# A third recursion level for two more products in one pair of round P2, and three pairs of stores moved between DMA queues

## The chip, the cores and the metric

The kernel runs on one core of a Trainium2 chip. The time is device microseconds of one execution, and the median of several executions is what counts. The engines are named as in the profile: PE is the matrix engine (PEld its weight loads), DVE the vector engine, ACT the scalar engine, POOL the GpSimd engine, and SP the engine that only issues DMA transfers and waits. SP and ACT issue DMAs into queues of their own. An engine works through its instructions in program order, so an instruction that waits holds everything behind it on that engine.

## The reference

All arithmetic is float32, for 32 samples `x[b]` of 128 channels by 2048 positions:

```python
att   = softmax(mlp(cond_128))                          # (32, 8)
x0    = einsum('boi,bih->boh', att @ weight, x) + bias   # a mixed 128x128 kernel per sample
x     = x + x0 @ W.T + bias + sum_e w_e (x0 @ A_e.T) @ B_e.T   # 2048 x 2048, low-rank update
x2    = grouped_conv1d(x, 9 taps) + ctx
x     = x + unperm(down(gelu(up(perm(x2)))))             # 16 heads, 128 -> 512 -> 128
```

The low-rank update is folded into the weights, so that the largest product is 4096 rows (samples times channels) by a 2048 x 2048 weight. The change is within this product.

## The kernel before

**The big product** is done with the Winograd form of Strassen's algorithm, which needs seven products of half-size blocks instead of eight. There are two levels everywhere and a third level in places.

- The outer level is the order of work: seven **rounds** `ROUNDS = ("P1", "P2", "P6", "P7", "P5", "P3", "P4")`. A round runs over eight groups of samples, `g = 0..7`; one round and one group is a **step** (`i` counts steps). Steps 2p and 2p+1 are **pair** p. In a step the left operand is a block of `x` (or a sum of blocks, made on POOL by `x_combine`, tiles `xt` and `s_P`), and the right operand is a block of the weights (`w` or `wo_P`, and sums `P_t` of it, made by `inner_weights`).
- The second level is within a step: again seven products P1 to P7, each of four matmuls with a 128 x 128 stationary block and 512 moving columns. Each float32 matmul is two passes of PE, and the profile counts passes.
- The third level takes the inner products of the two steps of a pair together, as seven **quarter** products, each of four matmuls of 256 columns. `multiply_third` does this for the inner products P2 and P4 (one family of quarters): each step has five full products (P1, P5, P6, P3, P7), and the seven quarters stand in the odd step. `multiply_more` does it for P3 and P7 as well (a second family): each step has three full products (P1, P5, P6), four quarters stand in the even step and ten in the odd one.

`PAIRS` says which pairs of a round use the third level at all, and `MORE` which of them use it for the second family also. Per pair, the matmuls are thus:

| | full matmuls (512 columns) | quarter matmuls (256 columns) |
|---|---|---|
| `multiply_third` | 2 x 5 x 4 = 40 | 7 x 4 = 28 |
| `multiply_more` | 2 x 3 x 4 = 24 | 14 x 4 = 56 |

**What a second family costs on other engines.** `more_weights` makes two tiles `P_v` of weight sums, eight operations on POOL at the step ahead of the pair (L471), and eight on DVE (L1321), of which one is taken at each of the first four calls of `between` in two steps. `more_inputs` makes a tile `sv` of sums of `s_P` tiles, four operations on POOL (L481 to L484). Each quarter of the second family is added to the results by two DVE instructions instead of one:

```python
part = acc[:, :, n, cols]
nc.vector.tensor_tensor(part, ps.rearrange("p (s n) -> p s n", s=2), part, ALU.add)   # L538
if n:                                   # second family
    part = acc[:, 1, 0, cols]
    nc.vector.tensor_tensor(part, ps[:, NQ : 2 * NQ], part, ALU.add)                  # L543
```

**Between the products** of a step the function `between(j)` is called for j = 0 to 5. It places other DVE work there, above all the **mixes**: the 256 operations (32 samples by 8 experts) that make the mixed kernels `ags` (L725, L727). `MIXES[r][g]` is how many are placed at each of j = 0 to 3, so a 2 means eight in the step. They must add up to 64. Small work of the conditioning network (`small`, L1049 to L1176) is spread over the steps by `next(chain)`; its softmax is L1074 to L1083, with an Exp on ACT (L1078) in the middle of a DVE sequence, and it is placed at the end of step 3 of round P1.

**Round P1** has no earlier sums to add to: ACT copies the first results from PSUM (L602), DVE adds the others, and at the end of a pair the two result tiles `m_P` (1 MB each) are stored to `p_d`. The same round finishes the weights (`w_make_two`, L232 to L235): before each of its first six steps' products there are PE products with DVE sums on top, stored by ACT (L177).

**The order on the DMA queues** is the program's order. The queue of SP holds all loads of `x` (L277), of partial sums (`part_load`, L282) and of weights (L173, L688), and the stores of partial sums (`part_store`, L286) of every round but the first. Loads of `x` stand one step ahead in the first round and two steps ahead later. All large tiles share 26 slots of 8 KB per partition (pool `big`); a load waits until the slot that it gets has been let go.

Of the kernel before, what the change touches and what calls it, by code (L numbers as in the profile page):

```python
# [51 lines left out]
    "P1": (0, 1, 2, 3), "P2": (0, 1, 2, 3), "P6": (0, 1, 2, 3), "P7": (0, 1, 2, 3),  # L52
    "P5": (0, 1, 2, 3), "P3": (0, 1, 2, 3), "P4": (0,),
}
MORE = {"P6": (1,), "P7": (1, 2, 3), "P3": (1, 2, 3)}
MIXES = {
    "P1": (0, 0, 0, 0, 0, 0, 2, 5),
    "P2": (0, 2, 2, 2, 2, 2, 2, 2),
    "P6": (0, 2, 1, 2, 2, 2, 2, 2),
    "P7": (0, 2, 1, 2, 1, 2, 2, 1),  # L60
    "P5": (0, 0, 0, 1, 1, 2, 2, 2),
    "P3": (0, 2, 1, 2, 1, 2, 2, 1),
    "P4": (0,) * 8,
}
# [5 lines left out]
def adaln_ffn_kernel(  # L70
# [16 lines left out]
    nc = tc.nc  # L87
# [8 lines left out]
    def slot(name, shape=(P, L)):  # L96
        return big.tile(list(shape), FP, name=name, tag="s")


    def bank():  # L100
        return banks.pop(0)

    def done(*ps):
        banks.extend(ps)

    def halves(t):
        return [t[:, r * NQ : (r + 1) * NQ] for r in range(2)]
# [177 lines left out]
    def part_store(n, g, t, eng=nc.gpsimd):  # L285
        eng.dma_start(part_d[n, g], t.rearrange("p k s c -> p (k s c)"))  # L286
# [164 lines left out]
    def sums_rest(eng, n=4):  # L451
        for _ in range(min(n, len(rest))):
            eng.tensor_tensor(*rest.pop(0))

    def more_weights(name, rhs):

        quarters, ops = [], []
        for i, k in enumerate(("P3", "P7")):
            t = slot(f"{name}_v{i}", (P, 4, 2, NQ))
            q = {"P1": [], "P2": [], "P3": [], "P4": [], "P5": [], "P6": [], "P7": []}  # L460
            for kc in range(2):
                (r11, r12), (r21, r22) = (halves(rhs[k][2 * h + kc]) for h in range(2))
                for n, r in zip(q, (r11, r21, r22, t[:, 3, kc], t[:, 0, kc], t[:, 1, kc], t[:, 2, kc])):
                    q[n].append(r)
                ops += [
                    (t[:, 0, kc], r12, r11), (t[:, 1, kc], r22, t[:, 0, kc]),
                    (t[:, 2, kc], r22, r12), (t[:, 3, kc], r21, t[:, 1, kc]),
                ]
            quarters.append(q)
        for op in ops[:8]:  # L470
            nc.gpsimd.tensor_tensor(*op, ALU.subtract)  # L471
        return quarters, ops[8:]

    def more_inputs(i):

        (x11, x12), (x21, x22) = (
            [ss[n][:, 2:4, h * NQ : (h + 1) * NQ] for h in range(2)] for n in (i, i + 1)
        )
        tt = nc.gpsimd.tensor_tensor
        t = slot(f"sv_{i}", (P, 4, 2, NQ))  # L480
        tt(t[:, 0], x21, x22, ALU.add)  # L481
        tt(t[:, 1], t[:, 0], x11, ALU.subtract)
        tt(t[:, 2], x11, x21, ALU.subtract)
        tt(t[:, 3], x12, t[:, 1], ALU.subtract)  # L484
        return {
            "P1": x11, "P2": x12, "P3": t[:, 3], "P4": x22,
            "P5": t[:, 0], "P6": t[:, 1], "P7": t[:, 2],
        }

    def in_more(r, g):  # L490
        return g // 2 in MORE.get(r, ())

# [95 lines left out]
    def multiply_third(r, g, lhs, rhs, olds, between, quarters, sq):  # L588

        px, py = bank(), bank()  # L590
        accs = olds if olds[0] is not None else [slot(f"m_{r}{g}", (P, 2, 2, QW))]
        fresh = set()
        if sq:
            both = [held.pop(), accs]

        def add(si, oi, ps):
            for acc in accs:
                to = acc[:, si, oi]
                if olds[0] is not None or (si, oi) in fresh:
                    nc.vector.tensor_tensor(to, ps, to, ALU.add)  # L600
                else:
                    nc.scalar.copy(to, ps)  # L602
            fresh.add((si, oi))

        def product(k, ps, first, last):
            for kc in range(4):
                nc.tensor.matmul(  # L607
                    ps, lhsT=lhs[k][:, bass.ts(kc, P)], rhs=rhs[k][kc],
                    start=first and kc == 0, stop=last and kc == 3, skip_group_check=True,
                )  # L610

        def quarter(k, to):

            if k in ("P1", "P5", "P2"):
                qs[k] = bank()
            ps = qs[{"P6": "P1", "P7": "P1", "P4": "P1", "P3": "P5"}.get(k, k)]
            first, last = k in ("P1", "P2", "P5"), k in ("P2", "P3", "P4")
            for i, out in enumerate(halves(ps)):
                for kc in range(2):
                    nc.tensor.matmul(  # L620
                        out, lhsT=sq[k][:, i, bass.ts(kc, P)], rhs=quarters[i][k][kc],
                        start=first and i == 0 and kc == 0, stop=last and i == 1 and kc == 1,
                        skip_group_check=True,
                    )
            b, h = to
            for acc in both[b]:
                part = acc[:, :, 0, h * NQ : (h + 1) * NQ]
                nc.vector.tensor_tensor(
                    part, ps.rearrange("p (s n) -> p s n", s=2), part, ALU.add
                )  # L630
            if last:
                done(ps)

        qs = {}
        turns = [
            (("P1", (0, 0)), ("P2", (0, 0))), (("P6", (0, 1)), ("P5", (1, 1))),
            (("P7", (1, 1)), ("P3", (0, 1))), (("P4", (1, 0)),),
        ]

        def turn(n, now):  # L640
            if sq and now:
                for k, to in turns[n]:
                    quarter(k, to)

        early = r not in ENDS
        product("P1", px, True, False)
        add(0, 0, px)
        between(0)
        turn(0, early)
        if sq:  # L650
            sums_rest(nc.vector)
        product("P5", py, True, False)
        add(1, 1, py)
        between(1)
        turn(1, early)
        product("P6", px, False, False)
        add(0, 1, px)
        between(2)
        turn(2, early)
        product("P3", py, False, True)  # L660
        add(0, 1, py)
        done(py)
        between(3)
        turn(3, early)
        product("P7", px, False, True)
        add(1, 1, px)
        add(1, 0, px)
        done(px)
        turn(0, not early)
        between(4)  # L670
        turn(1, not early)
        turn(2, not early)
        between(5)
        turn(3, not early)
        if not sq:
            held.append(accs)
            return
        for b, accs in enumerate(both):
            for (_, new), acc in zip(ADDED[r], accs):
                part_store(new, g - 1 + b, acc, nc.scalar if r == "P1" else nc.sync)  # L680

    held = []

# [552 lines left out]
    for i, (r, g) in enumerate(steps):  # L1236
        ri = i // NG
        last_round = ri + 1 == len(ROUNDS)
        if i + 1 < len(steps):
            if i + 1 not in xs:  # L1240
                xs[i + 1] = x_loads(*steps[i + 1])
            if not last_round:
# [8 lines left out]
                if in_more(r, g) and g % 2 == 0:  # L1251
                    sv = more_inputs(i)
                if r in MORE and g == 2 * MORE[r][0] - 1:
                    more, more_ops = more_weights(r, rhs)
# [91 lines left out]
        if in_more(r, g):  # L1346
            multiply_more(
                r, g, lhs.pop(i), rhs, olds.pop(i), between, ((quarters, sq), (more, sv))
            )
        elif in_pair(r, g):  # L1350
            multiply_third(
                r, g, lhs.pop(i), rhs, olds.pop(i), between, quarters, sq if g % 2 else None
            )
        else:
            multiply(r, g, lhs.pop(i), rhs, olds.pop(i), between)
# [105 lines left out]
```

## Time and profile before

| | us |
|---|---|
| median of three executions | 2571.3 (2570.91 to 2572.54) |
| profiled execution | 2569.07 |
| its span, first to last instruction | 2567.3 |
| PE busy in the span | 2556.8, in 7238 passes |
| DVE busy | 1616.1 |
| POOL busy | 1411.2 |
| ACT busy | 532.2 |
| HBM traffic over the span | 224 GB/s |

The page gives the busy time of each engine, the share of it in 40 slices, the DMA queues and the costliest groups of instructions. The busy time of PE includes the overlap of pipelined passes, so that the pace of PE is better read from the starts of instructions in the timeline: the start of one row to the start of the next. Times in the text are microseconds from the start of the span. Round P1 ends at about 295, round P2 covers 295 to 481, and its pair 2 (steps 4 and 5) 388 to 435.

### The profile page before, as it was taken

Reading aid. Unit: us, or ns where it says so; the run is one execution under the profiler, and the core shown is the slowest. Engines: PE = TensorE matmul, PEld = TensorE weight load, DVE = VectorE, ACT = ScalarE, POOL = GpSimd, SP = SyncE. Lnnn points to the kernel's source line nnn. Section 1 sums busy time; section 2 is a strip of 40 time slices with the busy share of each in tenths; the row PEclk is TensorE's granted clock in tenths of the full one; section 3 lists DMA queues with packets and bytes.
Section 4 is the critical chain, followed back from the end, with each engine's and each line's share of the span. In section 5 each row is a group of like instructions: output and inputs, shape, how many; then the busy total and the mean of one; then the engine's idle time right before and its main releaser. Section 6 shows DMA issues by size and latency. Waiting matters only on the chain. (4 is left out here: it accounts for less than half of the span.)

```text
span 2567.3 us, 22404 instructions
## 1 busy us (share of the span) xinstructions
PE 2556.8 (100%) x7238; PEld 1373.6 (54%) x7238; DVE 1616.1 (63%) x2505; ACT 532.2 (21%) x1099; POOL 1411.2 (55%) x1170
## 2 busy tenths in 40 slices
PE   9999999999999999999999999999999999999999
PEld 4555555565566555566554455455554554455543
DVE  5575566777776658766477666666666666666601
ACT  0000000000000000000011344444444444444432
POOL 8433677879997836989532144434334434434222
PEclk9999999999999999999999999999999999999999
DMA  8553688569466586574876987777777787787532
GB/s 344 195 187 117 242 322 313 210 267 392 150 248 265 202 340 264 230 287 165 285 237 202 298 297 248 224 251 235 230 218 239 246 251 222 222 250 239 163 125 90
DMA packets 186868, 610.44 MB, mean 238 GB/s; under 512 B 17664, under 2 KB 91904, under 8 KB 142336
## 3 DMA queue, kind: packets, MB, share of 16 engines
q1 hardware_dynamic: 146784, 465.09, 51.0%
q0 software_dynamic: 31264, 119.56, 14.1%
q10 hardware_dynamic: 8704, 24.37, 2.5%
q8 instruction: 58, 0.95, 0.1%
q14 instruction: 58, 0.48, 0.1%
HBM read 372.45 MB, written 202.94 MB: 224 GB/s over the span
## 5 line engine op out<-in xcount | busy, mean ns | idle before, releaser
L999 PE MATMUL bank<-t,ws 128*128 128x512 f32 x1024 | 460.3, 592 | 0.0
L1010 PE MATMUL bank<-gl,ws 128*128 128x512 f32 x1024 | 460.2, 592 | 0.0
L1017 POOL DMA_INDIRECT out<-t,orow x128 | 151.3, 1182 | 545.5 <-DVE t L1015 488.1
L1002 ACT ACTIVATE gl<-bank 128x512 f32<-128x512 f32 x512 | 306.2, 598 | 433.1 <-PE bank L999 430.6
L1010 PEld LDWEIGHTS bank<-gl,ws 128*128 128x128 f32 x1024 | 194.6, 190 | 233.0 <-issue 231.5
L999 PEld LDWEIGHTS bank<-t,ws 128*128 128x128 f32 x1024 | 194.6, 190 | 226.6 <-issue 223.4
L1015 DVE TENSOR_TENSOR t<-bank,t 128x512 f32<-128x512 f32 x128 | 88.4, 690 | 322.0 <-PE bank L1010 322.0
L748 POOL TENSOR_TENSOR x<-x,fb 128x512 f32<-128x512 f32 x128 | 174.2, 1390 | 182.8 <-DMA x<-in_x 133.8
L754 ACT ACTIVATE bank<-w,aggb 128x512 f32<-128x512 f32 x128 | 80.8, 684 | 877.5 <-DMA w<-w_d 865.3
L607 PE MATMUL bank<-P_t,s_P 128*128 128x512 f32 x576 | 255.7, 592 | 0.4 <-ACT m_P L602 0.4
L292 POOL TENSOR_TENSOR xt<-xt,xt 128x512 f32<-128x512 f32 x120 | 156.3, 1334 | 97.7 <-DMA xt<-in_xT 78.8
L727 DVE SCALAR_TENSOR_TENSOR ags<-mix,att_bc,ags 128x128 f32<-128x128 f32 x224 | 200.1, 893 | 4.2
L607 PEld LDWEIGHTS bank<-P_t,s_P 128*128 128x128 f32 x576 | 109.3, 190 | 127.6 <-issue 122.2
L328 POOL TENSOR_TENSOR s_P<-xt 128x512 f32<-128x512 f32 x52 | 68.8, 1323 | 191.4 <-DMA xt<-in_xT 110.3
L983 POOL DMA_INDIRECT t<-hx_d,row x128 | 131.5, 1027 | 54.4 <-issue 25.6
L600 DVE TENSOR_TENSOR u<-bank,u 128x512 f32<-128x512 f32 x132 | 85.3, 685 | 101.9 <-PE bank L607 98.9
L607 PE MATMUL bank<-wo_P,s_P 128*128 128x512 f32 x320 | 142.1, 592 | 0.0
L866 ACT ACTIVATE cv<-bank,ctxb 128x128 f32<-128x128 f32 x256 | 73.0, 368 | 233.4 <-PE bank L855 233.4
L855 PE MATMUL bank<-va,tw_l 128*128 128x256 f32 x512 | 121.1, 379 | 0.0
L766 DVE TENSOR_TENSOR x<-bank,x 128x512 f32<-128x512 f32 x128 | 88.0, 690 | 52.4 <-PE bank L763 21.5
L855 PEld LDWEIGHTS bank<-va,tw_l 128*128 128x128 f32 x512 | 97.0, 190 | 40.9 <-issue 30.5
L600 DVE TENSOR_TENSOR p<-bank,p 128x512 f32<-128x512 f32 x84 | 56.6, 687 | 96.5 <-PE bank L607 94.1
(239 smaller groups left out, 4030.1 us busy)
## 6 DMA issues: line engine op xcount, KB each, us to landing
xt<-in_xT SPq DMA_DIRECT2D x84, 1024.0 KB, 10.3
u<-u_d SPq DMA_DIRECT2D x40, 1024.0 KB, 9.6
wo_P<-wb_d SPq DMA_DIRECT2D x36, 1024.0 KB, 12.3
u<-c_d SPq DMA_DIRECT2D x64, 512.0 KB, 7.0
x<-in_x SPq DMA_DIRECT2D x32, 1024.0 KB, 8.9
xg<-x SPq DMA_DIRECT2D x256, 128.0 KB, 5.1
hx_d<-x1t SPq DMA_DIRECT2D x32, 1024.0 KB, 6.6
hx_d<-ht SPq DMA_DIRECT2D x32, 1024.0 KB, 7.2
```

The source lines that it names most:

```text
L292: nc.gpsimd.tensor_tensor(out[:, i, j], a[:, i, j], b[:, i, j], op)
L600: nc.vector.tensor_tensor(to, ps, to, ALU.add)
L607: nc.tensor.matmul(ps, lhsT=lhs[k][:, bass.ts(kc, P)], rhs=rhs[k][kc], start=first and kc == 0, stop=last and kc == 3, skip_group_check=True,)
L727: nc.vector.scalar_tensor_tensor(ag, mix[:, k], att, ag, ALU.mult, ALU.add)
L748: nc.gpsimd.tensor_tensor(xt[:, f], xt[:, f], late["fb"][:, f], ALU.add)
L855: nc.tensor.matmul(out, lhsT=w[:, 2 * i + r], rhs=rhs, start=first and r == 0, stop=last and r == 1, skip_group_check=True,)
L983: nc.gpsimd.indirect_dma_start(out=t.rearrange("p k t -> p (k t)"), out_offset=None, in_=hx_d[g].rearrange("l k t -> l (k t)"), in_offset= ...
L999: nc.tensor.matmul(pu, lhsT=w[:, m * P : (m + 1) * P], rhs=t[:, 0], start=True, stop=True)
L1002: nc.scalar.activation(gl[m], pu, AF.Gelu)
L1010: nc.tensor.matmul(pd, lhsT=w[:, (MC + m) * P : (MC + m + 1) * P], rhs=gl[m], start=(m == 0), stop=(m == MC - 1),)
L1015: nc.vector.tensor_tensor(t[:, 1], pd, t[:, 1], ALU.add)
L1017: nc.gpsimd.indirect_dma_start(out=out, out_offset=bass.IndirectOffsetOnAxis(ap=orow[:, g, h : h + 1], axis=0), in_=t[:, 1], in_offset=None,)
```

## The change

1. `MORE` gets `"P2": (2,)`: pair 2 of round P2 goes through `multiply_more` instead of `multiply_third`, with `more_weights` in step 3 and `more_inputs` in step 4.
2. `MIXES` moves: step 4 of P2 has one mix per place instead of two (four operations fewer). In P5, steps 1 and 2 get one per place instead of none, and step 7 one instead of two.
3. In round P1, the two stores at the end of steps 1, 3 and 7 are issued by SP; those of step 5 stay on ACT. Before, all of them were issued by ACT. (The condition in the code names step 5 alone, so the last pair moves too, not only the first two.)

```diff
-MORE = {"P6": (1,), "P7": (1, 2, 3), "P3": (1, 2, 3)}
+MORE = {"P6": (1,), "P7": (1, 2, 3), "P3": (1, 2, 3), "P2": (2,)}
 MIXES = {
...
-    "P2": (0, 2, 2, 2, 2, 2, 2, 2),
+    "P2": (0, 2, 2, 2, 1, 2, 2, 2),
...
-    "P5": (0, 0, 0, 1, 1, 2, 2, 2),
+    "P5": (0, 1, 1, 1, 1, 2, 2, 1),
...
@@ multiply_third
         for b, accs in enumerate(both):
             for (_, new), acc in zip(ADDED[r], accs):
-                part_store(new, g - 1 + b, acc, nc.scalar if r == "P1" else nc.sync)
+                part_store(new, g - 1 + b, acc, nc.scalar if (r, g) == ("P1", 5) else nc.sync)
```

## The prediction

> **What bounds the kernel now.** I read the page's head, then the waits of PE, then PE's timeline. PE is the bound from end to end and runs at full granted clock:
>
> ```profile
> span 2567.3 us, 22404 instructions
> PE 2556.8 (100%) x7238; PEld 1373.6 (54%) x7238; DVE 1616.1 (63%) x2505; ACT 532.2 (21%) x1099; POOL 1411.2 (55%) x1170
> PEclk9999999999999999999999999999999999999999
> ```
>
> All that PE waits for, by the view of waits (total us, times, longest):
>
> ```profile
> PE bank L166 <- DVE warm L163: 1.5, 1, 1.5
> PE bank L232 <- DVE w L235: 1.3, 1, 1.3
> PE bank L525 <- DVE u L543: 1.0, 2, 0.5
> PE bank L525 <- DVE p L543: 0.4, 1, 0.4
> PE bank L607 <- ACT m_P L602: 0.4, 1, 0.4
> ```
>
> So only two things move the time: the number of passes, and new or removed gaps on PE. Adding up every start-to-start distance above a pass's normal pace gives 7.3 us of gaps in the whole span. That limits any gain: beyond fewer passes there is little to win, but much to lose.
>
> **Part 1, the third level in pair 2 of P2: passes.** It removes 16 full matmuls (32 passes of 512 columns) and adds 28 quarter matmuls (56 passes of 256). The pace stands in PE's timeline in round P7, where both kinds alternate (start, us, then the line):
>
> ```profile
> 772.00 3.62 PE L525 MATMUL bank<-wo_P,s_P 128*128 128x256 f32 x16
> 775.45 3.60 PE L510 MATMUL bank<-wo_P,xt 128*128 128x512 f32 x8
> 778.88 3.62 PE L525 MATMUL bank<-P_q,sq 128*128 128x256 f32 x16
> 782.34 3.60 PE L510 MATMUL bank<-P_t,s_P 128*128 128x512 f32 x8
> ```
>
> From start to start, 16 passes of 256 take 3.455 us (0.216 each) and 8 of 512 take 3.43 (0.429 each): half the columns, half the time. Removed: 32 x 0.429 = 13.73. Added: 56 x 0.216 = 12.10. Net **-1.63 us**. A whole pair says the same: 46.43 us with one family (345.07 to 391.50), 44.78 with two and no gap (1174.70 to 1219.48).
>
> [...]
>
> **Part 1: a new gap.** The quarters of the second family have two DVE sums each (L538 0.68, L543 0.41 us). In the odd step DVE falls behind, and the last quarter, which goes on in a bank that DVE still reads, has to wait:
>
> ```profile
> 799.57 1.89 PE L525 MATMUL bank<-wo_P,sv 128*128 128x256 f32 x8
> 801.88 1.99 PE L525 MATMUL bank<-P_v,s_P 128*128 128x256 f32 x8 [0.43 <-DVE u L543]
> 803.71 3.60 PE L510 MATMUL bank<-wo_P,xt 128*128 128x512 f32 x8
> ```
>
> The rows are 2.31 and 1.83 us apart instead of 1.73 each: a gap of 0.68. The seven pairs that run this way now have gaps of 0.69 (P6), 0.39, 0.68, 0 (P7), 0.32, 0.82, 0 (P3). The two without one have one mix per place in the odd step, the five others two. P2's step 5 has two, with one in the even step as the others have. So I take the mean of the five, **+0.59 us**; bounds 0.32 and 0.82.
>
> **Part 1: DVE and POOL.** DVE gets eight P_v sums at 1.02 us (L1321: 24.4 us for 24), seven more first sums at 0.685 and seven second ones at 0.41, and gives four mixes at 0.893 away: 8.2 + 4.8 + 2.9 - 3.6 = 12.3 us, about 4.1 in each of steps 3, 4 and 5. The stretches 365 to 391, 391 to 412 and 412 to 438 now have DVE busy 15.1 of 26, 15.3 of 21 and 15.0 of 26. The middle one becomes 19.4 of 21; worked through one by one, DVE ends step 4 some 2.6 us late, under the first product of step 5 (3.43 us). That hides it. POOL gets eight P_v sums at 0.75 and four sv sums at 1.30: 11.2 us. It is hidden by POOL's own waits for loads in this stretch (4.2 us at 375, 3.9 at 400, 3.9 at 409, 5.4 at 448, 10.9 at 495).
>
> **Part 1: slots.** P_v (two) and sv hold three of the 26 slots from step 3 to the end of step 5. By the instruction order of the changed program, with the releases at today's times, the load of x for step 7 (now issued at 396.3) waits until about 421, and those of the last weight chunk (405.6 to 419.3) until about 430. Their sums on POOL come some 10 us late. PE first needs that x at 452 and that chunk at 484, and POOL is level again at 495. Nothing on PE.
>
> **Part 2, the mixes** that move to P5 put 3.6 us on DVE in steps 1 and 2. The stretches 872 to 898 and 898 to 919 have 18.0 and 10.9 us busy. Step 5 of P5, at 22.7 of 26, has no gap, so 21.6 and 14.5 cost nothing.
>
> **Part 3, the stores, the gain.** The 1.3 us gap at L232 lies at the end of step 3 of P1. Here are ACT's, DVE's and PE's timelines around it:
>
> ```profile
> 174.21 2.06 ACTq L286 DMA_DIRECT2D p_d<-m_P  x2
> 176.29 1.28 ACT L1078 ACT_TABLE_LOAD   x1 [12.03 <-DVE small L1076]
> 177.59 0.21 ACT L1078 ACTIVATE small<-small 32x8 f32<-32x8 f32 x1
> ```
>
> ```profile
> 177.83 0.15 DVE L1079 TENSOR_REDUCE small<-small 32x1 f32<-32x8 f32 x1 [1.35 <-ACT small L1078]
> ```
>
> ```profile
> 175.21 3.70 PE L232 MATMUL bank<-bf_sb,a_sb 128*128 128x512 f32 x8
> 180.19 4.10 PE L232 MATMUL bank<-tb,sa 128*128 128x512 f32 x9 [1.28 <-DVE w L235]
> ```
>
> The second store waits for the pair's last sum, and the table load for Exp stands behind it. DVE waits 1.35 us for Exp, and PE for DVE. With the stores on SP the table load has nothing in front of it since the copy at 163.68, Exp starts when DVE has its input (176.48) and not at 177.59, and DVE goes on 1.04 us sooner. PE's gap (1.44 by starts) shrinks to 0.4: **-1.04 us**. Bounds: 0, if something else on DVE is next, and -1.44. The other ACT gap, 0.57 us at 254.5, stays, since it hangs on another store (L1106).
>
> [...]
>
> **Part 3, the cost.** On SP the stores wait for the pair's end, and all later loads with them. After step 1 (103 to 105) the x for step 3 is late by 10 us (now issued at 95.5, needed by PE at 145.6). After step 3 (174 to 176) the x for step 5 is late by 14 us (162.7, needed at 218.8), and two weight loads by 1.5 us or less. After step 7 it is most:
>
> ```profile
> 272.97 0.33 SPq L1123 DMA_DIRECT2D t<-in_toep  x1
> 276.41 0.33 SPq L277 DMA_DIRECT2D xt<-in_xT  x1
> 284.14 0.33 SPq L282 DMA_DIRECT2D p<-p_d  x1
> 286.76 7.20 SPq L277 DMA_DIRECT2D xt<-in_xT  x4
> ```
>
> All seven now start behind the stores (294.4 and 296.1), at 296.5 or later. The one at 276.41 is the x of P2's step 1, which PE takes at 312.33. Ahead of it stand 2 MB of stores and 0.75 MB; with its own, 3.75 MiB = 3.93 MB. The stretches 298 to 305 and 305 to 312 moved 394 and 365 GB/s, so at 380 it lands 10.4 us after 295, at about 306: 6 us to spare. POOL then makes its sums (5.1 us), and four sums of P_q (2.9) by 314; PE needs them at 319 and 322.7. The chain of x sums on POOL runs 10 to 14 us late through P2 and its closest need I find is 9 us off. I cost it at nothing; the cover is those 6 us.
>
> **Sum:** -1.63 + 0.59 - 1.04 = **-2.08 us**. The profiled execution, 2569.07 (1.8 around the span), becomes 2567.0; the median stands 2.2 above it, so 2571.3 becomes **2569.2**. With the bounds: -1.63 + 0.32 - 1.44 = -2.75 to -1.63 + 0.82 = -0.8, so 2568.5 to 2570.5, and 0.8 either way for the spread of the three runs. A difference of 0.2% (5.1 us) is about what a measurement of this kernel tells from none; the forecast lies inside it.
>
> **Rivals.**
> - *The x of P2's step 1 comes late: slower.* If the nine transfers from 294.4 on (8.75 MiB, 9.2 MB) share the engines instead of being served in turn, all land together, 24 us after 295, at about 320. PE then waits about 7.6 us at 312.33, and the time is 2576.8. It decides from a landing at 312.33. Against it: the loads issued at 292.3, 292.8 and 293.6 landed at 297.6, 302.3 and 307.4, in turn. Chance 0.13.
> - *DVE becomes late.* One DVE sum (L1319 at 309.71) took 4.98 us instead of 1.06, while POOL ran four sums from 309.21 to 314.14. POOL's work in P2 moves, and such a collision may fall where DVE has no slack: up to 4 us, 2569.2 to 2573.2. Chance 0.12.
> - *The Exp gap stays*, since DVE's backlog is next: 2570.3. Chance 0.12.
> - *Faster by more than 5.1 us.* No row offers it: passes and the whole L232 gap give 3.1. Chance 0.03.
>
> **Numbers.** Forecast 0.60, the rivals as given (0.40). Within 0.2%: 0.60 + 0.12 + 0.12 = 0.84, less 0.02 for a backlog of loads that I have missed: 0.82. Slower 0.15, faster 0.03. The range 2567.0 to 2574.0 takes the forecast with its bounds, the Exp rival and the DVE one.
>
> **What would show it.** Right: 7262 passes on PE; the pair takes about 45.4 us instead of 46.6; a gap of 0.3 to 0.8 at its last quarter, ended by L543; Exp at 176.5 and a gap at L232 of 0.4; no gap at 312. Wrong: a wait of PE for a DMA of `xt`, or for POOL's `s_P` or `P_q`, early in P2; a DVE sum of several us in steps 3 to 5; gaps in P5.

## The result and the profile after

The changed kernel takes **2574.43 us** (median of 22 runs, 2573.13 to 2578.61) against 2570.79 for the kernel before in the same runs (22 runs, 2569.15 to 2573.20). The ratio is 1.0016, with a 95% interval of 1.0010 to 1.0021: 3.6 us slower. The prediction held 0.2% to be about what a measurement of this kernel tells from none; with 22 runs each the interval is 2.6 to 5.4 us longer, so this is a difference. It lies 5.2 us above the forecast of 2569.2, on the other side of the time before, and 0.4 us outside the range.

The head of the page, in the order of before:

```profile
span 2572.3 us, 22493 instructions
...
PE 2556.9 (99%) x7262; PEld 1378.8 (54%) x7262; DVE 1626.0 (63%) x2527; ACT 532.9 (21%) x1099; POOL 1435.0 (56%) x1182
```

The passes are the 7262 that were forecast, the granted clock is 0.999 on average, and yet the span is 5.0 us longer. So PE waited more. The view of PE's waits (total us, times, longest) names it:

```profile
PE bank L620 <- DVE p L628: 5.8, 1, 5.8
PE bank L166 <- DVE warm L163: 1.5, 1, 1.5
```

One long wait is new, and it is longer than the five rows shown of before together (4.6). The other row is the old one of the start-up. PE's timeline shows where it is (start, us, then the line, and in brackets the idle time before it and what ended it):

```profile
364.52 3.60 PE L607 MATMUL bank<-P_t,s_P 128*128 128x512 f32 x8
373.92 5.20 PE L620 MATMUL bank<-P_q,sq 128*128 128x256 f32 x16 [5.81 <-DVE p L628]
378.96 3.60 PE L607 MATMUL bank<-P_t,s_P 128*128 128x512 f32 x8
```

Eight passes of 512 take 3.43 us, so the second row was due at about 367.95 and came at 373.92: 5.97 us. A second loss stands behind it: the 16 passes of that row take 5.04 us from start to start, where 3.455 is their pace, so 1.58 more. The view of windows gives the granted clock there (the third figure from the end):

```profile
364.50:370.00 5.50, 3.61 (x9) 1.33 (x7) 0.64 (x1) 0.00 (x0) 5.42 (x5) 1.00 1.01 429
370.00:377.00 7.00, 3.08 (x7) 2.52 (x8) 4.53 (x7) 0.00 (x0) 6.84 (x10) 0.51 0.98 410
377.00:383.00 6.00, 6.00 (x21) 3.79 (x20) 2.26 (x4) 0.00 (x0) 6.00 (x6) 1.00 0.21 48
```

While PE waits, its granted clock goes from 1.00 to a half (from about 370; the mean of 370 to 377 is 0.51), and it reads 1.00 again from 377.0. The seven passes up to there take 3.09 us, against 1.51 at their pace. So the place costs 5.97 + 1.58 = **7.55 us**.

This is step 3 of round P2, the step *before* the pair that was changed. PE waits there for a bank that DVE has not read. DVE's timeline says what held DVE:

```profile
363.11 2.03 DVE L727 SCALAR_TENSOR_TENSOR ags<-mix,att_bc,ags 128x128 f32<-128x128 f32 x2
372.33 0.85 DVE L1321 TENSOR_TENSOR P_v<-w 128x256 f32<-128x256 f32 x1 [7.19 <-DMA tw_d<-tw]
373.10 1.48 DVE L628 TENSOR_TENSOR p<-bank,p 128x512 f32<-128x512 f32 x2
```

The first of the new weight sums, the one that opens the second tile `P_v`, waits 7.19 us for a DMA that has nothing to do with weights: the store of `tw` to `tw_d`. The two sums L628 behind it on DVE, which free PE's banks, wait with it. `tw` is a tile of `small`'s chain: convolution weights, finished by DVE at L1138 and stored at L1139. It sits in one of the 26 slots of the pool `big`, and the new tile was given just that slot: the store landed at 372.2, and the tile's first write started at 372.33. The view of the tile itself (who waited for it, us, times) says it from the other end:

```profile
who waited for it (us, times):
  DVE P_v L1321: 7.2, 1
```

In the kernel before, nobody waited for this store. It also landed sooner there: 3.9 us after its issue at 363.04, against 9.6 us after 362.61 now. The reason stands on SP's timeline. First before, then after:

```profile
344.06 0.86 SPq L277 DMA_DIRECT2D xt<-in_xT  x1
345.02 2.32 SPq L688 DMA_DIRECT2D wo_P<-wb_d  x3
...
363.04 0.32 SPq L1139 DMA_DIRECT2D tw_d<-tw  x1
```

```profile
352.92 0.33 SPq L277 DMA_DIRECT2D xt<-in_xT  x1
354.53 1.82 SPq L688 DMA_DIRECT2D wo_P<-wb_d  x3
362.61 0.32 SPq L1139 DMA_DIRECT2D tw_d<-tw  x1
```

The four loads of 1 MB ahead of the store go out 9 us later, because the stores at the end of step 7 of P1 now stand ahead of SP's loads and the lateness is handed on through round P2. Before, these loads were through when the store came; now three of them are still to land. The view of windows shows it for the 5 us from 360 on, first before, then after (the last two columns are the DMA share and GB/s):

```profile
360.00:365.00 5.00, 5.00 (x19) 3.40 (x18) 4.93 (x6) 0.63 (x1) 5.00 (x4) 1.00 0.27 111
```

```profile
360.00:365.00 5.00, 5.00 (x21) 3.66 (x20) 4.93 (x6) 0.63 (x1) 4.92 (x5) 1.00 1.01 424
```

Over the store's own time, from issue to landing, the engines moved 326 GB/s before (363.04 to 366.94) and move 424 now (362.61 to 372.20). Its 1 MB is 269 GB/s of the first and 109 of the second. What is ahead of it can be read from the three loads of `wo_P` that SP issued from 354.53 to 355.84. This is their view in the changed kernel:

```profile
DMA to landing us min/median/max: 10.0/11.9/13.5
```

In order of issue they land at 364.6, 366.9 and 369.4, and the store comes next, at 372.2. SP's transfers land one after the other here, and the store has the loads in front of it.

### The profile page after: what moved, and what is told of

The parts are those of the page before. It is cut to its first block, busy times and chain, and to the rows that moved or that the text cites. A ratio compares the mean times of both kernels' runs of the same rounds, so it can differ in the third digit from the quotient of the medians.

```text
span 2572.3 us, 22493 instructions
## 1 busy us (share of the span) xinstructions
PE 2556.9 (99%) x7262; PEld 1378.8 (54%) x7262; DVE 1626.0 (63%) x2527; ACT 532.9 (21%) x1099; POOL 1435.0 (56%) x1182
## 5 line engine op out<-in xcount | busy, mean ns | idle before, releaser
L607 PE MATMUL bank<-P_t,s_P 128*128 128x512 f32 x544 | 241.4, 592 | 0.4 <-ACT m_P L602 0.4
L727 DVE SCALAR_TENSOR_TENSOR ags<-mix,att_bc,ags 128x128 f32<-128x128 f32 x224 | 193.4, 863 | 3.9
L607 PEld LDWEIGHTS bank<-P_t,s_P 128*128 128x128 f32 x544 | 103.3, 190 | 120.6 <-issue 115.4
L855 PE MATMUL bank<-va,tw_l 128*128 128x256 f32 x512 | 121.7, 380 | 0.7 <-DVE va L839 0.7
L855 PEld LDWEIGHTS bank<-va,tw_l 128*128 128x128 f32 x512 | 96.9, 190 | 42.3 <-issue 31.5
L763 PE MATMUL bank<-u,agl 128*128 128x512 f32 x256 | 115.1, 592 | 0.0
```

The source lines that it names most:

```text
L607: nc.tensor.matmul(ps, lhsT=lhs[k][:, bass.ts(kc, P)], rhs=rhs[k][kc], start=first and kc == 0, stop=last and kc == 3, skip_group_check=True,)
L727: nc.vector.scalar_tensor_tensor(ag, mix[:, k], att, ag, ALU.mult, ALU.add)
L763: nc.tensor.matmul(pm, lhsT=ag, rhs=u[:, f], start=False, stop=True, skip_group_check=True)
L855: nc.tensor.matmul(out, lhsT=w[:, 2 * i + r], rhs=rhs, start=first and r == 0, stop=last and r == 1, skip_group_check=True,)
```

## The theory and its rivals

**Theory.** Part 1 and part 3 of the change are each harmless and cost 7.55 us only together. The third level brings a tile whose slot hangs on the store of `tw` (part 1), and the late loads make that store slow (part 3). **Rival 1:** the late loads alone cost the time. **Rival 2:** DVE simply has too much work in steps 3 to 5, wherever the tile lies. **Rival 3:** the store is slow because of its place in SP's queue, not because of the traffic.

The edits below are to the changed kernel, unless they say otherwise. The first four experiments shared runs of the kernel before (2570.33, 33 runs), and the last two did (2570.64, 21 runs); each median of an experiment is of 11 runs.

### The third level alone

```diff
-part_store(new, g - 1 + b, acc, nc.scalar if (r, g) == ("P1", 5) else nc.sync)
+part_store(new, g - 1 + b, acc, nc.scalar if r == "P1" else nc.sync)
```

> Third level and mixes as changed, all stores of round P1 on ACT as before. Slot theory (the first P_v sum on DVE waits because its tile gets the slot of tw, and the store of tw lands late behind loads that the stores on SP have delayed): here the loads are on time, tw's store lands at about 366.9 as before, DVE waits under 2 us for it, and PE has a gap of 0.3 to 0.8 us near 367. With 1.6 us fewer passes and the 1.4 us gap at L232 still there: 2569.5 to 2570.4 against 2570.8 of before. Rival 1 (the late sums of x on POOL hold PE or DVE, whatever the slot): no gap near 367, 2569.2. Rival 2 (DVE has simply too much to do in step 3): the gap of 6.5 us stays, 2575.7.

Measured: **2568.71** (2567.47 to 2571.23), ratio 0.9994 (0.9985 to 1.0003). DVE waits for the same store, but for 1.71 us instead of 7.19, since it ends 4.0 us after the store's issue at 365.74:

```profile
369.70 0.42 DVE L1321 TENSOR_TENSOR P_v<-w 128x256 f32<-128x256 f32 x1 [1.71 <-DMA tw_d<-tw]
```

PE has no gap there: DVE's lead covers 1.7 us. So the slot's wait is there without part 3, only short. The gap of 0.3 to 0.8 us that was expected near 367 did not come, and the time lies 0.8 us below the expected range, less than its interval can tell. By its time this run would fit rival 1 as well (2569.2); the wait for the store is what rival 1 does not have.

### The stores alone

To the kernel before, this makes the change of the stores alone:

```diff
-part_store(new, g - 1 + b, acc, nc.scalar if r == "P1" else nc.sync)
+part_store(new, g - 1 + b, acc, nc.scalar if (r, g) == ("P1", 5) else nc.sync)
```

> Only the stores of steps 1, 3 and 7 of round P1 on SP; third level and mixes as before. Slot theory: the loads of round P2 are as late as in the changed kernel, but no P_v tile waits for tw, so PE has no gap near 367; the 1.4 us gap at L232 is gone: 2569.2 to 2569.6. Rival 1 (late sums of x): a gap of about 6 us near 367, 2575.4. Rival 2 (DVE's work): no gap, 2569.4.

Measured: **2569.26** (2568.95 to 2570.91), ratio 0.9996 (0.9987 to 1.0005). The loads are as late as in the changed kernel and the traffic from 360 to 365 as full (423 GB/s), but without the tile `P_v` nobody waits for the store, and PE has no gap near 367. Rival 1 falls: by it the time would be 2575.4. Of the late loads only a gap of 0.4 us at 354 is left.

### Step 7's stores back on ACT

```diff
-nc.scalar if (r, g) == ("P1", 5) else nc.sync
+nc.scalar if (r, g) in (("P1", 5), ("P1", 7)) else nc.sync
```

> The changed kernel, but the stores of step 7 of round P1 on ACT again (steps 1 and 3 stay on SP). Slot theory: loads of P2 on time, DVE waits under 2 us for tw's slot, gap of PE near 367 of 0.3 to 0.8, no gap at L232; passes -1.6, L232 -1.4: 2568.0 to 2569.0, with up to 0.6 more if the gap at the pair's last quarter comes back when POOL is on time. Rival 1: 2567.7. Rival 2: the 6.5 us gap stays, 2574.3.

Measured: **2567.67** (2565.16 to 2570.20), ratio 0.9988 (0.9979 to 0.9997). The loads go out at 342.6 to 345.9 again, DVE's wait is 1.71 us, and PE goes on at its pace:

```profile
364.26 3.60 PE L607 MATMUL bank<-P_t,s_P 128*128 128x512 f32 x8
367.70 3.62 PE L620 MATMUL bank<-P_q,sq 128*128 128x256 f32 x16
```

The same two rows that stood 9.40 us apart in the changed kernel stand 3.44 apart. Of part 3, then, the stores of the last pair, those of step 7, did the harm. The gap of 0.3 to 0.8 us that was expected near 367 did not come here either, and the time is 0.3 us below the expected range. This run alone does not tell the theory from rival 1, by which it would be 2567.7; the run of the stores alone does.

### Another slot for the tile, the loads as late

```diff
 # more_weights, ahead of its sums on POOL
+if name == "P2":
+    nc.vector.tensor_tensor(*ops.pop(8), ALU.subtract)
```

The first write of the second tile moves to the start of step 3, so that it should take a slot that had been free for long. Who gets the slot of `tw` instead no view shows; nobody waits for its store in this kernel.

> The changed kernel, but the first of the eight P_v sums on DVE stands at the start of step 3 instead of behind its first product, ahead of the sums on POOL, so that its tile takes a slot that is free since 342; tw's slot goes to a load of weights. Loads of P2 as late as in the changed kernel. Slot theory: no gap near 367, 2567.6 to 2568.4. Rivals 1 and 2: the gap of 6.5 us stays, 2574.4.

Measured: **2567.37** (2566.57 to 2569.38), ratio 0.9989 (0.9980 to 0.9998). DVE has the same sums to make in the same steps, the traffic is as full (431 GB/s from 360 to 365), and the sum waits for nothing:

```profile
363.79 1.49 DVE L471 TENSOR_TENSOR P_v<-w 128x256 f32<-128x256 f32 x1
```

The time is 0.2 us below the expected range. Rival 2 falls: it was not the amount of DVE's work but which slot one instruction wrote to. In this kernel the gap at the pair's last quarter appears (more on it below).

### Both cures

The two edits together. If each cured a loss of its own, they would add up.

> The two cures together: the stores of step 7 of round P1 on ACT again, and the first P_v sum on DVE at the start of step 3 so that it does not get tw's slot. If the slot's wait is the whole loss, either cure takes all of it and the two together add nothing but the 0.3 us gap near 354, which only the kernels with late loads had: 2567.0 to 2567.8 with 2570.3 for before. If late loads cost something of their own besides the slot, this one is over 1 us faster than the early sum alone: 2566.3 or less.

Measured: **2567.40** (2566.53 to 2568.64), ratio 0.9988 (0.9979 to 0.9997). They do not add up: one loss, with two conditions. Against their own runs of the kernel before, the two cures together are at -3.2 us, the early sum alone at -3.0 and the stores of step 7 alone at -2.7. The difference of the parts says the same: the third level alone is at -1.6 us, the stores alone at -1.1, together they would be -2.7, and the change is at +3.6. The 6.3 us between are what the two cost only together. Each of these medians has an interval of 1.4 to 2.3 us to either side, so that 6.3 and the 7.55 of the one profile do not contradict each other.

### The store of `tw` on ACT's queue

```diff
-nc.sync.dma_start(tw_d, tw.rearrange("p k r c -> p (k r c)"))
+nc.scalar.dma_start(tw_d, tw.rearrange("p k r c -> p (k r c)"))
```

> The changed kernel with one instruction moved: the store of tw is issued by ACT instead of SP, so that it does not stand behind the four loads that SP issued before it; the loads themselves are as late as in the changed kernel. If the place in SP's queue makes the store late (9.6 us to its landing instead of 3.9), it lands at 366 to 368 now, and the gap near 367 falls from 6.5 us to between 0 and 1.3: 2567.5 to 2569.5. If the traffic of the loads makes it late, whichever queue it stands in, the gap stays at 5 us or more: 2572.5 to 2574.5.

Measured: **2575.07** (2573.76 to 2576.57), ratio 1.0019 (1.0010 to 1.0028): nothing is won. ACT issues the store at 362.80, and DVE can go on at 372.10, 9.3 us later; from SP it was 372.33:

```profile
362.80 0.33 ACTq L1139 DMA_DIRECT2D tw_d<-tw  x1
```

```profile
372.10 0.58 DVE L1321 TENSOR_TENSOR P_v<-w 128x256 f32<-128x256 f32 x1 [6.78 <-DMA tw_d<-tw]
```

Rival 3 falls so far as it says that the store would land sooner from another queue. It does not follow that order plays no part. On SP's queue the store landed behind the loads, as shown above; how it shared the engines with the loads from ACT's queue no view shows. What the two have in common is the traffic of the late loads: the engines moved 424 GB/s over the store's time from SP, and 423 to 424 in the three stretches of 5 us from 360 to 375 with the store on ACT. PE's wait of 5.12 us is again followed by slow passes: the first six take 2.90 us, against 1.46 at pace (an estimate: five times 0.216 from start to start, and 0.379 for the last). The granted clock is 0.79 in the stretch from 370 to 375, where it is 1.00 from 350 to 370.

## Why the prediction was right or wrong

**The passes: right.** The count is 7262, and pair 2 takes 44.77 us from its first pass to the next step's (394.44 to 439.21), against 46.56 before (388.06 to 434.62), which held 0.15 of gaps. The forecast of 1.63 less is 1.64. By the medians the third level alone is at -1.6 us, with an interval of -3.9 to +0.8.

**The new gap at the last quarter: +0.59 forecast, nothing measured.** PE went through it at pace, 1.73 us apart, and DVE's mixes beside it were short:

```profile
432.30 1.89 PE L525 MATMUL bank<-P_v,sv 128*128 128x256 f32 x8
434.03 1.89 PE L525 MATMUL bank<-P_q,xt 128*128 128x256 f32 x8
```

```profile
433.11 0.73 DVE L727 SCALAR_TENSOR_TENSOR ags<-mix,att_bc,ags 128x128 f32<-128x128 f32 x2
```

Two mixes take 0.73 us here. POOL was idle from 429.8 to 437.7, waiting for PE to let go of a tile. In the kernel with the tile in another slot POOL was at work until 431.1, two mixes at 428.65 took 2.33 us, and the gap came back:

```profile
431.97 1.35 PE L527 MATMUL bank<-P_v,s_P 128*128 128x256 f32 x5 [0.58 <-DVE p L545]
```

The term took the mean of five pairs (0.58, not 0.59) and compared their counts of mixes. In these kernels the gap goes with the length of a mix, and that with POOL: with the third level alone and with step 7's stores back on ACT there is no gap either, and POOL waits 12.00 and 11.98 us for PE there. With both cures there is no gap. No run changed POOL's work alone, so this cause is argued.

**The gap at L232: -1.04 forecast, -1.44 measured.** It is gone altogether, in the changed kernel and with the stores alone. ACT loads its table 12 us early and Exp starts when its input is there:

```profile
164.30 1.28 ACT L1078 ACT_TABLE_LOAD   x1
176.40 0.21 ACT L1078 ACTIVATE small<-small 32x8 f32<-32x8 f32 x1 [10.81 <-DVE small L1077]
```

It starts at 176.40, 0.08 before the forecast, and not at 177.59. The step was right; the 0.4 us of rest that it left is missing because DVE gained more than the wait. DVE goes on at 176.64 instead of 177.83, 1.19 us sooner, and its instruction at L1081 takes 0.22 us instead of 0.72, so that the first sum of L235 starts at 177.67 instead of 179.37. Why L1081 was shorter no run shows.

**The cost of the stores on SP: right where it was worked out.** The stores and the loads behind them go out at

```profile
292.90 2.05 SPq L286 DMA_DIRECT2D p_d<-m_P  x2
295.04 0.69 SPq L1123 DMA_DIRECT2D t<-in_toep  x1
295.82 1.16 SPq L277 DMA_DIRECT2D xt<-in_xT  x1
```

and the `x` for P2's step 1 lands at 304.8 (306 was forecast). There is no gap at 312, and the first rival of the prediction has not come. No PE wait for `xt`, `s_P` or `P_q` arose in P2, with POOL late as forecast. The mixes in P5 cost nothing, as forecast.

**The slots: the step that failed.** The paragraph says of `P_v` and `sv`: they "hold three of the 26 slots", follows the loads that must wait longer for a slot, and closes with "Nothing on PE". It asked who waits because the new tiles hold slots. It did not ask what the new tiles themselves wait for. The paragraph was costed at nothing and measured +7.55 us in the profile: 5.97 of waiting for the store of `tw`, and 1.58 of slow passes behind the wait, at a granted clock of 0.50 (373.92 to 377.0). By the medians the cures win back 6.3 to 6.9 us. The row was within reach: the store of `tw` issued at 363.04 and landing 3.9 us later, and a new tile asked for at about 365. Even with that row the sum would have said "1.7 us, hidden", as the runs of the third level alone show; the 7.2 needs the late loads too, which the prediction had in another paragraph and followed only to PE and POOL, not to the store that stands behind those loads.

**The sum,** with what was measured by the gaps of the two profiles: -1.64 for the passes, 0 at the last quarter, -1.44 at L232, +7.55 for the slot, and +0.38 for a gap at 353.4 that all kernels with late loads have: +4.85 us. The spans differ by 5.0, and the rest are small gaps that come and go from profile to profile (the start-up, the last quarters in P6, P7 and P3, and L855 near 1405). The medians differ by less, 3.6, since the profiled execution of before (2569.07) was 1.7 us faster than its median of 2570.79, and that of the changed kernel (2574.19) only 0.2.

**The rivals.** "DVE becomes late" named the right engine, with a price of up to 4 us. The cause that it gave, a collision with POOL, was not the one. The listed sign for "wrong", a DVE sum of several us in steps 3 to 5, is nearly what the trace shows: not a long sum, but a long wait ahead of one.

## What to carry to other kernels

A new tile in a shared pool has a price of its own: find the instruction that first writes it, the old tile whose slot it gets, and the last reader of that. Here this reader was a DMA store: the wait of 7.19 us ended 0.1 us after the store had landed (372.2), and the two sums L628 behind the writing instruction on DVE waited too. A long wait of PE can cost more than its length: here 5.97 us of waiting had 1.58 us of slow passes behind it, at a granted clock of 0.50. Two edits that shift traffic and slots should be weighed together: here both cures, another slot for the tile or one pair of stores left on ACT, make the kernel 3.0 and 2.7 us faster than before, where the change as it stood made it 3.6 slower.

## What the runs showed of the hardware that was not expected

**PE's clock was down behind a long wait, and the passes there paid again.** Behind a wait of 5.81 us the granted clock was 0.50 until 3.1 us after PE went on, and the passes of 256 columns took about 0.44 us (seven in 3.09) instead of 0.216: 1.58 us on top of the wait. With the store on ACT's queue six passes took 2.90 us, against 1.46 at pace, behind a wait of 5.12 us, and the clock was 0.79 from 370 to 375. In the kernel before, in which no wait of PE is longer than 1.5 us, the clock reads 1.00 from 10 to 2560 us, and in the first four experiments, with no wait over 1.8 us, it reads 1.00 from 350 to 375. No run took the wait and the clock apart.

**From another queue the store landed about as late.** The same 1 MB store took 3.9 us while the engines moved 326 GB/s, and, with the loads late, 9.6 us at 424 GB/s (from SP) or 9.3 at 423 to 424 (from ACT, to the end of DVE's wait).

**DVE's mixes took longer while POOL made sums.** Two mixes took 0.73 us with POOL idle (433.11 in the changed kernel) and 2.33 with POOL at work (428.65 with the tile in another slot). In one place of the changed kernel they took 5.31 us, about as long as POOL's four sums beside them (the 0.38 us gap of PE at 353.4 stands right behind):

```profile
348.13 5.31 DVE L727 SCALAR_TENSOR_TENSOR ags<-mix,att_bc,ags 128x128 f32<-128x128 f32 x2
```

```profile
347.97 4.93 POOL L292 TENSOR_TENSOR xt<-xt,xt 128x512 f32<-128x512 f32 x4
```

The length here is that of four instructions of POOL in a row and not of one (1.2 us); what decides that no run here shows.
